# A fused attention and gated FFN kernel: VectorE in written order through the projections, powers instead of reciprocals, other places for pieces of work

## The chip, the cores and the metric

The kernel runs on one core of one Trainium2 chip. The metric is the device time of one execution in microseconds (us); below 1% differences matter here, since the kernel takes some 1,100 us. The core has five engines that run their own instruction streams and wait for each other by semaphores: TensorE (PE, with its weight loads as PEld), VectorE (DVE), ScalarE (ACT), GpSimd (POOL) and SyncE (SP, which here only issues DMAs). Tiles lie in SBUF as 128 partitions by some elements; matmul results land in PSUM banks of 128x512 floats.

## What is computed

```python
x   = hidden_states                      # (B, S, E) = (4, 512, 1024), float32
xn  = (x - mean) / sqrt(var + 1e-5)      # layernorm without gain
# attention: 16 heads of 64, rotary on all 64 dimensions, causal
q, k = rotary(xn @ Wq), rotary(xn @ Wk); v = xn @ Wv
attn = softmax(where(causal, q k^T, -1e9) / 8)
s    = (attn v) @ Wo
# gated FFN with signs of weights and scales chosen by a router over 8 experts
r    = softmax(xn @ gate_w^T)            # (B*S, 8)
out  = (xn * (r @ in_channel_scale)) @ sign(weight)^T * (r @ out_channel_scale) + bias
g    = silu(out)
result = x + s * g
```

## The kernel before

**Tiling.** Batches b = 0 to 3 go one after the other. The heads of a batch form 4 groups g, a group two units, `u = (b, g, i)` with i = 0, 1, of two heads each. For each group six tiles of 128 columns x 512 rows are projected: q and k of unit 0, q and k of unit 1, v of both. Their running number is the position `pos`, 24 to a batch. To keep float32 accuracy with the fast matmul type, an operand is split into two digits (high and low), and a tile is 24 products of 128x512 in three passes of eight: high weights by high x (`xh`), low by low (`xl`), and a mixed pass, `wm` by `xm`. The products are L364 in `passes`. The first 16 go to one PSUM bank, which ScalarE copies to `part` (L339), the last 8 to a second; VectorE adds both into `c` (L418; L414 for the last tile of a batch, which has another order). The projections' banks come from a ring of four. So a tile's bank is free again once ScalarE or VectorE has read it. From q and k the rotary embedding (`rotary`, L325 and L326 on VectorE, L327 and L328 on GpSimd) makes `rot`; v is transposed on TensorE (`turn_values`, L347, tile `vt`).

**Weights.** In batch 0 the raw float32 weights are loaded (`load_w`, issued by ScalarE, `wr<-in_wqkv`), and `digits_w` makes the high digit on ScalarE (step 0, L299), the low one on VectorE (step 1, L301), writes both to `w_d` in DRAM (issued by SyncE), and makes `wm` (step 2, L316 on VectorE; for odd positions from 13 to 23 L311 on ScalarE and L312 on GpSimd). Later batches load both digits from `w_d` (issued by GpSimd, L280, three buffers), and only `wm` is made again. `beside(n)` in `project` places these steps behind the n-th product of a tile.

**Beside the products.** A group has 144 products, and `interleave` calls "pieces" ahead of the products whose numbers are their keys. The pieces do the attention of the group before (`attention_pieces`): `scores` (L476), `softmax` (VectorE adds the mask and takes the maximum, L493; ScalarE takes the exponentials and their row sums, L505; VectorE their reciprocals, L514; GpSimd scales the rows, L516), `transpose_blocks` (ten VectorE transposes, L534, into a staging tile `y` that has one buffer, and 16 small DMAs `p<-y` issued by SyncE, L544, which bring it into the place of the probabilities), `values` (L559) and the store of its result, `at_d<-v`. Unit 0's scores stand at product 24, unit 1's at 96. In the last group of batch 3 the attention of the group before has places of its own. The pieces also do, for the next batch, the layernorm (`layernorm_scales` L174 and on, `normalize`), the transposes of x and their digits (`transpose_x`, `high_x` on ScalarE, `low_x` L238 on VectorE, `mixed_x`), the router (`router_tile`, `router_turn`, `router`), once in batch 0 the load and split of the FFN's scales `isc` and `osc` (`load_scales`, `split_scales`, L660 to L668), and in batch 3 the signs of the FFN's weights (`make_sign`).

**What sets the order.** TensorE runs in written order throughout (`manual_schedule(engines={PE})`); VectorE and ScalarE only in the start, before the first group. Elsewhere the scheduler of the framework orders the instructions of an engine when the program is built, but for those marked `keep_in_program_order`. On the chip each engine runs its stream in that built order, and an instruction that waits holds all behind it.

**After the groups** come the last units' attention, the FFN and the output projection (products L1156 and L1216), some 340 us. There `load_xn` loads normalized rows back by SyncE and, in four small loads by GpSimd each, the router's weights `RT` for a pair of row tiles; its first call stands in group 1 of batch 3.

## Time and profile before

| what | value |
|---|---|
| time, median of 3 runs | 1114.22 us (1111.3 to 1115.96) |
| profiled execution: its time, its span | 1117.55 us, 1115.8 us |
| mean granted TensorE clock | 0.986 |
| PE, PEld busy | 1069.3 us (96%), 734.8 us (66%) |
| DVE busy, instructions | 871.3 us (78%), 1857 |
| ACT busy, instructions | 391.1 us (35%), 931 |
| POOL busy, instructions | 548.9 us (49%), 642 |
| start to the first product of group 0 | 28.5 us |
| batch 0: groups 0 to 3 | 31.5, 48.1, 56.0, 60.3 us |
| batch 1 | 44.5, 43.4, 48.7, 49.0 us |
| batch 2 | 44.4, 43.4, 49.4, 47.5 us |
| batch 3 | 45.8, 45.5, 45.6, 46.0 us |
| after the last product | 777.5 to 1115.8 us |

A group's time goes from its first product of L364 to the next group's. (Group 0 of batch 0 has only four of its six tiles; the other two are made in the start.) Busy time of PE is modelled from pipelined matmuls, and it holds work at a lower clock too: the granted clock, 1.00 at full speed, says how much of a stretch PE ran at which speed. "x <- ENGINE y" behind an instruction gives its idle time and what ended it. An engine's waits cost time only where the engine is on the path that ends last; for this kernel that is, most of the time, PE's stream of products.

### The profile page before, as it was taken

Reading aid. Unit: us, or ns where it says so; the run is one execution under the profiler, and the core shown is the slowest. Engines: PE = TensorE matmul, PEld = TensorE weight load, DVE = VectorE, ACT = ScalarE, POOL = GpSimd, SP = SyncE. Lnnn points to the kernel's source line nnn. Section 1 sums busy time; section 2 is a strip of 40 time slices with the busy share of each in tenths; the row PEclk is TensorE's granted clock in tenths of the full one; section 3 lists DMA queues with packets and bytes.
Section 4 is the critical chain, followed back from the end, with each engine's and each line's share of the span. In section 5 each row is a group of like instructions: output and inputs, shape, how many; then the busy total and the mean of one; then the engine's idle time right before and its main releaser. Section 6 shows DMA issues by size and latency. Waiting matters only on the chain.

```text
span 1115.8 us, 15662 instructions
## 1 busy us (share of the span) xinstructions
PE 1069.3 (96%) x4948; PEld 734.8 (66%) x4948; DVE 871.3 (78%) x1857; ACT 391.1 (35%) x931; POOL 548.9 (49%) x642
## 2 busy tenths in 40 slices
PE   9897988899999999999999999999999999999998
PEld 8675665577776667776677766766654546655664
DVE  5989867787877898678888989978775876667663
ACT  4243645333343433324444223343530222222220
POOL 1545665644755546555464644654552333432334
PEclk9898989999999999999999999999999999999999
DMA  8686767898678787777778787686665223431331
GB/s 303 249 313 182 277 210 258 270 290 248 193 208 267 227 258 205 218 228 211 251 230 233 230 258 243 202 233 197 209 183 188 88 72 123 155 115 51 141 113 57
DMA packets 86530, 228.37 MB, mean 205 GB/s; under 512 B 14640, under 2 KB 37936, under 8 KB 74032
## 3 DMA queue, kind: packets, MB, share of 16 engines
q1 hardware_dynamic: 67408, 129.71, 37.7%
q0 software_dynamic: 15344, 85.60, 23.7%
q10 hardware_dynamic: 3696, 12.06, 3.1%
q8 instruction: 40, 0.66, 0.2%
q14 instruction: 42, 0.34, 0.1%
HBM read 134.77 MB, written 50.59 MB: 166 GB/s over the span
## 4 chain that ended last, share of the span: by engine, by line
PE 38%; DVE 22%; DMA 14%; SPq 8%; issue 5%; POOL 3%; ACT 3%; DVEq 0%; ACTq 0%; POOLq 0%
PE wo L1216 15%; PE pj L364 11%; SPq L544 7%; DVE y L534 7%; PE ff L1156 6%; DMA w<-w_d 5%; DMA p<-y 4%; DVE wm L316 3%; PE pv L559 2%; DMA at_d<-v 2%; DVE sc L493 2%; POOL p L516 2%; PE sc L476 2%; DVE c L418 2%; DVE rot L325 2%
## 5 line engine op out<-in xcount | busy, mean ns | idle before, releaser
L364 PE MATMUL pj<-xm,wm 128*128 128x512 f32 x752 | 202.5, 404 | 12.0 <-DVE c L418 7.2
L364 PE MATMUL pj<-xh,w 128*128 128x512 f32 x752 | 198.1, 404 | 5.6 <-DVE xl L238 4.9
L364 PE MATMUL pj<-xl,w 128*128 128x512 f32 x752 | 193.8, 396 | 0.0
L327 POOL TENSOR_TENSOR c<-c,sin_sb 128x512 f32<-128x512 f32 x64 | 89.1, 1392 | 208.7 <-DVE c L326 202.8
L516 POOL TENSOR_SCALAR p<-p,rs 128x256 f32<-128x256 f32 (+3 forms) x256 | 172.6, 686 | 34.9 <-DVE rs L514 23.6
L505 ACT ACTIVATE p<-sc,nmx 128x256 f32<-128x256 f32 (+3 forms) x256 | 133.3, 526 | 130.9 <-DVE nmx L493 73.9
L364 PEld LDWEIGHTS pj<-xh,w 128*128 128x128 f32 x752 | 140.2, 192 | 47.7 <-issue 8.8
L364 PEld LDWEIGHTS pj<-xm,wm 128*128 128x128 f32 x752 | 139.6, 192 | 43.7 <-DVE c L418 8.0
L316 DVE SCALAR_TENSOR_TENSOR wm<-w 128x1024 fp32r<-128x1024 f32 x88 | 128.0, 1454 | 44.7 <-DMA w<-w_d 24.7
L364 PEld LDWEIGHTS pj<-xl,w 128*128 128x128 f32 x752 | 140.5, 190 | 30.5 <-issue 1.6
L493 DVE CUSTOM_DVE_ANT_0 sc<-sc,mask 128x384 f32<-128x384 f32 (+3 forms) x256 | 121.4, 506 | 10.9 <-PE sc L476 9.1
L534 DVE STREAM_TRANSPOSE y<-p 128x256 f32<-128x256 f32 x320 | 107.9, 405 | 2.3 <-POOL c L327 1.2
L339 ACT ACTIVATE part<-pj 128x512 f32<-128x512 f32 x90 | 53.8, 598 | 146.6 <-PE pj L364 79.6
L328 POOL TENSOR_TENSOR rot<-rot,c 128x512 f32<-128x512 f32 x64 | 93.1, 1454 | 3.9
L559 PE MATMUL pv<-p,v 128*64 128x256 f32 (+3 forms) x512 | 79.1, 453 | 9.3 <-DMA p<-y 4.3
L476 PE MATMUL sc<-rot,rot 64*128 64x128 f32 (+3 forms) x512 | 79.5, 443 | 0.0
L559 PEld LDWEIGHTS pv<-p,v 128*64 128x64 f32 x512 | 36.4, 140 | 55.6 <-issue 40.4
L418 DVE TENSOR_TENSOR c<-pj,part 128x512 f32<-128x512 f32 x90 | 61.0, 678 | 12.8 <-PE pj L364 12.8
L280 POOL DMA_DIRECT2D w<-w_d x73 | 43.1, 590 | 53.6 <-PE pj L364 47.9
L476 PEld LDWEIGHTS sc<-rot,rot 64*128 64x128 f32 x512 | 42.4, 187 | 30.1 <-issue 21.0
L1216 PE MATMUL wo<-wo,ap 128*128 128x512 f32 x128 | 58.5, 599 | 0.0
L1236 POOL TENSOR_TENSOR xp_z<-xp_z,xr 128x512 f32<-128x512 f32 x16 | 22.8, 1423 | 66.9 <-DVE xp_z L1235 66.9
(186 smaller groups left out, 1582.4 us busy)
## 6 DMA issues: line engine op xcount, KB each, us to landing
w<-w_d POOLq DMA_DIRECT2D x73, 1024.0 KB, 6.3
p<-y SPq DMA_DIRECT2D x496, 80.0 KB, 2.7
w_d<-w SPq DMA_DIRECT2D x24, 1024.0 KB, 6.6
wr<-in_wqkv ACTq DMA_DIRECT2D x20, 512.0 KB, 5.5
at_d<-v SPq DMA_DIRECT2D x32, 256.0 KB, 5.4
ap<-at_d SPq DMA_DIRECT2D x16, 512.0 KB, 5.0
xr<-in_x SPq DMA_DIRECT2D x32, 256.0 KB, 2.9
xin<-in_x SPq DMA_DIRECT2D x12, 512.0 KB, 6.4
```

Of the source, the lines that this page charges most:

```text
L316: nc.vector.scalar_tensor_tensor(WM[key], low.bitcast(F32), -1.0 / LOW, hi.bitcast(F32), op0=ALU.mult, op1=ALU.add)
L327: nc.gpsimd.tensor_tensor(c, c, sin_sb, op=ALU.mult)
L328: nc.gpsimd.tensor_tensor(rot, rot, c, op=ALU.add)
L364: nc.tensor.matmul(ps, lhsT=wd[:, k, :], rhs=xd[:, k, :], start=(at == 0), stop=(at == n - 1),)
L418: nc.vector.tensor_tensor(c, second, p, op=ALU.add)
L476: nc.tensor.matmul(head(i, h), lhsT=Q[u][r : r + D, i * P : (i + 1) * P], rhs=K[u][r : r + D, : (i + 1) * P], start=True, stop=True,)
L493: nc.vector.tensor_tensor_reduce(out=ps[h], in0=ps[h], in1=mask[:, (TPB - 1 - i) * P :], scale=-SCALE, scalar=FAR, op0=ALU.add, op1=ALU.mi ...
L505: nc.scalar.activation(pt[:, h, :], ps[h], AF.Exp, bias=nmx[:, h : h + 1], scale=-1.0, accum_out=ssum[:, h : h + 1],)
L516: nc.gpsimd.tensor_scalar(pt[:, h, :], pt[:, h, :], rs[:, h : h + 1], 1.0, op0=ALU.mult, op1=ALU.mult,)
L534: nc.vector.transpose(out[:, :, :, o : o + 32], src.rearrange("p h (b c) -> p h b c", b=4))
L559: nc.tensor.matmul(by_block[r : r + D, :, 32 * j :], lhsT=V[u][:, j, r : r + D], rhs=PT[u][:, :, o : o + 32 * (TPB - j)], start=(j == 0), ...
L1216: nc.tensor.matmul(ps, lhsT=lhs[:, k, :], rhs=rhs[:, k, :], start=(first and k == 0), stop=(k == 3), skip_group_check=not first,)
```

## The change

The change has seven parts.

1. `interleave` of all groups runs under `manual_schedule(engines={DVE})`: VectorE's instructions of the projections keep the written order, with no scheduler. `beside` and the pieces are written accordingly: a tile's `c` is written right behind its last product; `ahead_of_scores` (rotary of the tile before, then `wm` of the next one) comes at the third product of a tile, or ahead of scores where these come first; `digits_w` steps 0 and 1 stay at 9 and 13; `mixed_x` goes to 10, 13, 16, 19.
2. `softmax` works on pairs of row tiles with a shared tile of row sums. Their reciprocals are no longer VectorE instructions, two to a pair, but one GpSimd power with exponent -1 over 128x4; the scaling follows for both tiles.
3. Places of attention: transposes of unit 1 at product 12 instead of 4, of unit 0 at 88 instead of 76 (last group 82 instead of 62), and in the last group those of unit 1 at 136 instead of 124.
4. Layernorm of the next batch: statistics and normalization of one tile at 8 and of the next at 62, instead of both statistics at 0 and normalization at 0 and 30; `low_x` comes 7 products behind its transposes.
5. The router's softmax is cut in two (steps 1 and 1.5) and its steps get other places.
6. The load and split of the scales move from group 1 of batch 0 (2, 52, 86) to group 0 of batch 1 (2, 66, 128).
7. The loads of `RT` keep the written order.

```diff
@@ -82,8 +82,9 @@
     nc.gpsimd.memset(eps, EPS)
-    power = cp.tile([P, 1], F32, name="power")
-    nc.gpsimd.memset(power, -0.5)
+    power = cp.tile([P, 2], F32, name="power")
+    nc.gpsimd.memset(power[:, 0:1], -0.5)
+    nc.gpsimd.memset(power[:, 1:2], -1.0)
@@ -180,7 +181,7 @@
         rstd = st.tile([P, 1], F32, tag="rstd", name=f"rstd_{b}_{t}")
         nc.gpsimd.tensor_tensor(rstd, mv[:, 1:2], eps, op=ALU.add)
-        nc.gpsimd.tensor_tensor(rstd, rstd, power, op=ALU.pow)
+        nc.gpsimd.tensor_tensor(rstd, rstd, power[:, 0:1], op=ALU.pow)
         MV[b, t] = mv, rstd
@@ -220,7 +221,6 @@
         if b > 0:
             high_x(b, t, g)
-            low_x(b, t, g)
         if g == 1:
@@ -348,8 +348,19 @@
             nc.scalar.copy(V[u], vt)
+    now = [0]
+    mixed = {2, 3}
+
+    def ahead_of_scores(pos):
+        while turn:
+            rotary(*turn.pop(0))
+        if pos + 1 not in mixed:
+            mixed.add(pos + 1)
+            digits_w(pos + 1, 2)
+
     def project(pos):
+        now[0] = pos
         key = b, g, m, i = keys[pos]
@@ -375,19 +386,16 @@
                 if pos + 2 == 23:
                     load_w(24)
-            if n == 3 and turn:
-                rotary(*turn.pop(0))
+            if n == 3:
+                ahead_of_scores(pos)
             if n == 20:
                 turn_values()
-            if last and b + 1 < B and n in (10, 12, 14, 16):
-                mixed_x(b + 1, (10, 12, 14, 16).index(n))
+            if last and b + 1 < B and n in (10, 13, 16, 19):
+                mixed_x(b + 1, (10, 13, 16, 19).index(n))
             if pos in (4, 5) and n in (6, 10):
                 digits_w(pos - 4, (6, 10).index(n))
-            if pos + 2 < 24:
-                if n in (9, 13, 18):
-                    digits_w(pos + 2, (9, 13, 18).index(n))
-            elif n == 12:
-                digits_w(pos + 2, 2)
+            if pos + 2 < 24 and n in (9, 13):
+                digits_w(pos + 2, (9, 13).index(n))
@@ -482,8 +490,12 @@
     def softmax(u, *tiles):
+        if len(tiles) > 2:
+            softmax(u, *tiles[:2])
+            return softmax(u, *tiles[2:])
         un = "%d_%d_%d" % u
-        for i in tiles:
+        ssum = st.tile([P, 2, 2], F32, tag="ssum", name=f"ssum_{un}_{tiles[0]}")
+        for n, i in enumerate(tiles):
             pt, ps = probs(u, i), SC[u, i]
@@ -500,7 +512,6 @@
                     accum_out=nmx[:, h : h + 1],
                 )
-            ssum = st.tile([P, 2], F32, tag="ssum", name=f"ssum_{un}_{i}")
             for h in range(2):
@@ -508,13 +519,16 @@
                     bias=nmx[:, h : h + 1],
                     scale=-1.0,
-                    accum_out=ssum[:, h : h + 1],
-                )
-            rs = st.tile([P, 2], F32, tag="rs", name=f"rs_{un}_{i}")
-            nc.vector.reciprocal(rs, ssum)
+                    accum_out=ssum[:, n, h : h + 1],
+                )
+        nc.gpsimd.tensor_tensor(
+            ssum, ssum, power[:, 1:2, None].to_broadcast((P, 2, 2)), op=ALU.pow
+        )
+        for n, i in enumerate(tiles):
+            pt = probs(u, i)
             for h in range(2):
                 nc.gpsimd.tensor_scalar(
-                    pt[:, h, :], pt[:, h, :], rs[:, h : h + 1], 1.0,
+                    pt[:, h, :], pt[:, h, :], ssum[:, n, h : h + 1], 1.0,
                     op0=ALU.mult, op1=ALU.mult,
@@ -610,6 +624,10 @@
             )
             nc.scalar.activation(exv, exv, AF.Exp)
+            R["ex"] = ex
+        elif step == 1.5:
+            ex = R["ex"]
+            exv = ex[:, :, :NE]
             ssum = st.tile([P, TPB], F32, tag="rsum", name=f"rsum_{b}")
@@ -627,7 +645,6 @@
             for n in (1, 0):
                 nc.vector.tensor_copy(ex[:, :, n * NE : (n + 1) * NE], hi)
-            R["ex"] = ex
         else:
@@ -698,9 +715,11 @@
         RT[q] = rtp.tile([P, 2, P], F32R, tag="rt", name=f"rt_{q}")
         for j in range(4):
-            nc.gpsimd.dma_start(
-                out=RT[q][32 * j : 32 * j + 32, :, :],
-                in_=rt_d[b, t : t + 3 : 2].rearrange("t e p -> e t p"),
+            tc.keep_in_program_order(
+                nc.gpsimd.dma_start(
+                    out=RT[q][32 * j : 32 * j + 32, :, :],
+                    in_=rt_d[b, t : t + 3 : 2].rearrange("t e p -> e t p"),
+                )
             )
@@ -835,6 +854,7 @@
                 if before:
                     values(before)
+                ahead_of_scores(now[0] + 1)
                 scores(u)
@@ -844,15 +864,15 @@
         last = k == len(groups) - 2
         plan = {
-            4: lambda: v and transpose_blocks(v),
+            12: lambda: v and transpose_blocks(v),
             24: values_and_scores(w, u0),
             32: lambda: softmax(u0, 2, 0),
-            62 if last else 76: lambda: transpose_blocks(u0),
+            82 if last else 88: lambda: transpose_blocks(u0),
             72 if last else 96: values_and_scores(v, u1),
...
         }
         if last:
-            plan[124] = lambda: transpose_blocks(u1, ordered=True)
+            plan[136] = lambda: transpose_blocks(u1, ordered=True)
         return {n: [piece] for n, piece in plan.items()}, units
@@ -876,25 +896,27 @@
                         at(n + 14 * (t // 2), lambda f=f, t=t: f(0, t))
             else:
-                at(56, lambda: router(b, 1))
+                at(44, lambda: router(b, 1))
+                at(54, lambda: router(b, 1.5))
                 at(74, lambda: router(b, 2))
+            if b == 1:
+                at(2, lambda: (load_scales(in_scale), load_scales(out_scale)))
+                at(66, lambda: split_scales(isc))
+                at(128, lambda: split_scales(osc))
         elif g == 1 and b + 1 < B:
             at(100, lambda: [load_x(b + 1, t) for t in range(2)])
             if b == 0:
-                at(2, lambda: (load_scales(in_scale), load_scales(out_scale)))
-                at(12, lambda: router(0, 1))
-                at(34, lambda: router(0, 2))
-                at(52, lambda: split_scales(isc))
-                at(86, lambda: split_scales(osc))
+                at(10, lambda: router(0, 1))
+                at(20, lambda: router(0, 1.5))
+                at(44, lambda: router(0, 2))
         elif g > 1 and b + 1 < B:
             t0 = 2 * (g - 2)
-            layernorm_scales(b + 1, t0)
-            layernorm_scales(b + 1, t0 + 1)
-            normalize(b + 1, t0)
-            at(30, lambda: normalize(b + 1, t0 + 1))
+            for n, t in ((8, t0), (62, t0 + 1)):
+                at(n, lambda t=t: (layernorm_scales(b + 1, t), normalize(b + 1, t)))
             for n, t, h in ((46, t0, 0), (56, t0, 1), (108, t0 + 1, 0), (116, t0 + 1, 1)):
                 at(n, lambda t=t, h=h: transpose_x(b + 1, t, h))
+                at(n + 7, lambda t=t, h=h: low_x(b + 1, t, h))
             at(78, lambda: router_tile(b + 1, t0))
@@ -915,7 +937,8 @@
             if g == 2:
                 at(8, lambda: in_scales(0, score_banks))
-        interleave(pieces, fill, 0 if k else 2 * 3 * NC, 6 * 3 * NC)
+        with tc.manual_schedule(engines={DVE}):
+            interleave(pieces, fill, 0 if k else 2 * 3 * NC, 6 * 3 * NC)
         if g == NGRP - 1:
             for _ in fill:
                 pass
```

## The prediction

> **What bounds the kernel now.** First I read the windows, cut at each group's first projection product (L364): below, groups 1 to 3 of batch 0, then groups 0 to 3 of batch 1, 144 products each. Columns: stretch, its length, busy time of PE, PEld, DVE, ACT and POOL with counts, granted clock, DMA share, GB/s.
>
> ```profile
> core 0: us, PE busy (x) PEld busy (x) DVE busy (x) ACT busy (x) POOL busy (x), PEclk, DMA share, GB/s
> 59.90:108.00 48.10, 42.42 (x186) 32.44 (x185) 44.97 (x91) 18.95 (x44) 27.52 (x29) 0.93 0.71 239
> 108.00:164.00 56.00, 50.53 (x250) 36.01 (x250) 44.60 (x99) 30.54 (x66) 35.97 (x37) 0.94 0.76 248
> 164.00:224.30 60.30, 51.44 (x267) 36.50 (x266) 45.60 (x100) 27.99 (x61) 33.53 (x36) 0.94 0.78 255
> 224.30:268.80 44.50, 44.50 (x236) 32.82 (x235) 36.64 (x98) 15.29 (x44) 25.26 (x31) 1.00 0.84 261
> 268.80:312.20 43.40, 43.40 (x218) 32.37 (x217) 33.16 (x84) 14.85 (x42) 24.36 (x30) 1.00 0.77 225
> 312.20:360.90 48.70, 47.54 (x251) 34.48 (x250) 39.50 (x95) 20.96 (x53) 25.97 (x36) 1.00 0.75 232
> 360.90:409.90 49.00, 48.06 (x268) 34.44 (x267) 41.87 (x99) 21.29 (x54) 25.77 (x35) 1.00 0.76 233
> ```
>
> The same products take 164.4 us in batch 0 (first three rows) and 141.1 in batch 1 (last three), with the clock at 0.93 to 0.94 against 1.00. From batch 1 on, PE is the bound: products start 0.227 us apart (48 in 10.9 us in the chain). Next, what PE waits for between 59 and 224:
>
> ```profile
> PE pj L364 <- DVE c L418: 7.2, 2, 5.7
> PE pj L364 <- DVE xl L238: 5.8, 2, 3.1
> PE pv L559 <- DMA p<-y: 4.3, 1, 4.3
> ```
>
> With three smaller rows (1.4, 0.7, 0.7) that is 20.1 us. Columns are sum, times, longest. The timeline of DVE shows what stood ahead of the sum c in the longest wait, 91.9 to 97.5:
>
> ```profile
> 93.85 0.71 DVE L666 TENSOR_SCALAR xin<-xin,row_kind 128x1024 f32<-128x1024 f32 x1
> 94.48 1.22 DVE L316 SCALAR_TENSOR_TENSOR wm<-w 128x1024 fp32r<-128x1024 f32 x1
> 95.61 1.28 DVE L668 SCALAR_TENSOR_TENSOR osc<-osc,row_kind,xin 128x1024 fp32r<-128x1024 f32 x1
> 96.81 0.68 DVE L418 TENSOR_TENSOR c<-pj,part 128x512 f32<-128x512 f32 x1
> ```
>
> The split of the scales and the next-but-one wm run first (ten transposes, 3.36 us, before them); the tile's last pass was long done. So in batch 0 PE waits for the order on DVE, not for its capacity: DVE is busy 44.6 of 56.0 and 45.6 of 60.3. From 224 to 750 PE waits only 8.9 us in all, 4.9 of them vt for c.
>
> **The change, part by part.** Sums are made in the profiled execution (1117.55 us, span 1115.8, 1.75 outside it) and taken off the median, 1114.22; the 3.3 between them I leave alone.
>
> *Batch 0, groups 1 to 3.* Three things leave DVE or move. The split, 0.69+0.75+2.29 for isc, 0.68+0.71+1.28 for osc and 0.45 of row kinds, 6.85 us, leaves group 1. The reciprocals leave: in all 128 of 163 ns with 40.1 us of waiting in front of them, of which the sum behind an eviction waits too. c comes ahead of wm (1.2 to 1.5 us). In written order transposes of unit u1 (piece 12) also stand before the next softmax; before, DVE did the one at 184.33 after it, its 16 transfers were issued up to 203.5 and the value product waited 4.3. Floors: PE as in batch 1, 43.4 less two value products of 2.3 that group 1 hasn't, 38.8, then 48.7 and 49.0, sum 136.5; DVE 44.97-6.85-1.2=36.9, 43.3, 44.3, lower in each. Ceiling 164.4-136.5=28. That agrees with the 20.1 of waits plus the half clock: five rows of 25 us from 75 to 225 show 0.93, 0.94, 0.86, 0.93, 0.93, that is 0.41x25=10.2 us. But both engines are nearly full, w L301 still waits for raw weights (w L301 <- ACT w L299, 4.1 in one wait at 101), and DVE now can't step around that. I take two thirds, **18** (8 to 28).
>
> On the clock: each PE wait of 2.6 us or more up to 224 (5.7, 2.6, 3.1, 4.3) is followed by 3.4 or 6.8 us at 0.50; after 830 a wait of 2.57 is too. *The Trainium skill, "TensorE: Matmul & The Clock Gate", section HAM oscillation, warns of idle gaps above about 3.4 us alone; by it only the 5.7 and the 4.3 would cost clock, 5 of the 10.2 us; here shorter waits cost too, and the row decides.*
>
> *Powers on GpSimd.* Two for each unit, 64. No 128x4 power is in the trace; nearest row rstd L183, 128x1, 556 ns. Lower bound 0.556, upper four times that; I take 0.6, 38 us in all, 2.4 of the 43 to 60 of a group where POOL is busy 24 to 36. Queued behind one: the scaling L516, rotary's L327 and L328, and weight loads w<-w_d. Scaling now waits for two tiles' exponentials, some 1.7 us later; the cover is that transposes of u0 stand at product 88 instead of 76, 56 products or 12.7 us after the second softmax. At the upper price 4 powers add 9 us to a group's POOL, 35 of 43: still hidden, save 1 us a group if loads slip (0 to 13, taken 0).
>
> *The Trainium skill, "SBUF — State Buffer", section Who interferes with whom, says that a VectorE instruction with two SBUF inputs and a GpSimd one that reads SBUF block each other for the whole instruction. The trace agrees in kind: isc L668 took 2.29 us beside a busy POOL and osc L668 1.28. By the rule at its worst the 38 us of powers would all be added to DVE, 2.4 a group; the windows leave DVE 7 to 10 there, so the sum stays as it is.*
>
> *Batch 1, group 0* takes the split: DVE 36.64+6.85-1.2=42.3 of 44.5. Two loads of 0.5 MB (4 us at 261 GB/s) go on SP ahead of p<-y and at_d there. Cost 0 to 4, taken 1.
>
> *Other groups.* wm(pos+1) now comes after c, rotary's two DVE steps and before the scores. DVE waited 19.2 us in 10 times with wm for PE (224 to 750), each with the sum behind it; those end. low_x seven products after its transposes and statistics one tile at a time remove head waits of 1.5 us. Of the 8.9 us that PE waited I take 4 (0 to 9).
>
> *The loads of rt* (8 on POOL, 0.56 each) move from 77 us to batch 3 and the tail: 2.2 us each where POOL idles (11.1 us before 787). Taken 0 (-1 to 1).
>
> *The last group* goes the wrong way. Transposes of u0 move from product 62 to 82, behind the second softmax; those of u1 from 124 to 136. Both write one staging tile y, freed when its 16 transfers have landed. Before:
>
> ```profile
> 758.49 3.38 DVE L534 STREAM_TRANSPOSE y<-p 128x256 f32<-128x256 f32 x10
> ...
> 762.01 10.09 SPq L544 DMA_DIRECT2D p<-y  x16
> ...
> 774.83 3.38 DVE L534 STREAM_TRANSPOSE y<-p 128x256 f32<-128x256 f32 x10 [1.18 <-POOL c L327]
> ...
> 779.18 0.66 PE L347 MATMUL vt<-ident,c 128*128 128x128 f32 x4 [1.31 <-DVE c L414]
> ```
>
> Start to start 16.3 us, with 1.18 of idling. After: scores end at 760.8, two softmaxes 3.6 us (starts 743.62 to 748.94 less 1.7 of waits), so u0's transposes start at 764.5 and u1's not before 780.8; ten of them 3.3, then the last sum c 0.7, which stands behind: vt at 784.8 instead of 779.2. 5.6 us, and by the rows above some 1.7 us of half clock. I take **7** (0 to 9).
>
> Sum: -18+1-4+7 = -14; 1114.2-14 = **1100**.
>
> **The rivals.** *All waits go* (A): batch 0 reaches its floor (-28), other groups -8, last group +3: 1081. For: DVE has room in every row. Against: written order makes every late input a late sum.
>
> *Batch 0 is held by its loads* (B): the raw weights (5.5 us landing, DMA share 0.71 to 0.78) set L301, L301 the sum. Then only the split and some reciprocals count, -8, others 0, last +7 and +1: 1114, no change. For: w L301 <- ACT w L299 and wr<-in_wqkv in the chain (195.9, 5.2 us). Against: batch 1 moves as many GB/s without waits.
>
> *The staging tile holds DVE in every group* (C, slower): u0's transposes at 88 and u1's at 12 are 68 products apart, 15.4 us plus 4.7 of value product and scores, 20.1. A cycle takes 3.4+transfers+2.7 landing. From 14.0 us of transfers on, DVE stands with the sum behind it. Rows: 10.1 to 11.0 in batch 3, 15.8 once in batch 0. If 15.8 holds everywhere, 1.8 us in each of 26 unit turns, half of it reaching PE with its clock, 27: 1114-14+27=1127.
>
> *It doesn't take effect* has no place: the built order differs on DVE from the third projection on.
>
> **How the numbers follow.** Forecast 0.55 (own range 1090 to 1109), A 0.15, B 0.18, C 0.12. The range 1084 to 1116 takes in the forecast, a little of A and most of B. A measurement here tells about 0.5%, 5.6 us, from no change: faster is A, nearly all of the forecast and a third of B, 0.76; same 0.13; slower C's most, 0.11.
>
> **What would show it.** Right: groups 1 to 3 of batch 0 take some 146 us, with PEclk 1.00 in most of 75 to 225; no split at 80 to 97 but in batch 1; vt <- c of about 6 us at the end of the projections, half clock after it. Wrong: DVE idle before L301 in batch 0 (B); y L534 <- DMA p<-y on DVE in many groups (C); no vt wait at the end (A, or my cycle of y is too long); powers far above 0.6 us with POOL the bound.

## The result, and the profile after

The changed kernel takes 1162.66 us (median of 4 runs, 1162.05 to 1165.88) against 1114.20 of the kernel before: ratio 1.0443, 95% interval 1.0414 to 1.0473. The change makes it 4.4% slower; the prediction was 1100, and its range ended at 1116. In the profiled execution the span is 1160.8 us against 1115.8, the mean granted clock 0.976 against 0.986. DVE is as busy as before (871.9 us against 871.3), POOL much busier: 656.2 against 548.9.

Where the 45.0 us went is read from the first products (now L375) of the groups and a few later marks of TensorE's stream, which has nearly the same order in both kernels:

| stretch, us | before | after | difference |
|---|---|---|---|
| batch 0 | 195.9 | 194.4 | -1.5 |
| batch 1 | 185.5 | 192.9 | +7.4 |
| batch 2 | 184.8 | 189.7 | +4.9 |
| batch 3 | 182.9 | 196.8 | +13.9 |
| last product to last vt | 1.7 | 6.4 | +4.7 |
| vt to first product of the output projection | 54.1 | 56.6 | +2.5 |
| from there to the last product | 278.0 | 290.8 | +12.8 |

Table and windows come from one execution of each kernel. The windows of the changed kernel at the same places as in the prediction: groups 1 to 3 of batch 0, then 0 to 3 of batch 1 (columns as there).

```profile
core 0: us, PE busy (x) PEld busy (x) DVE busy (x) ACT busy (x) POOL busy (x), PEclk, DMA share, GB/s
57.50:103.70 46.20, 42.48 (x186) 31.95 (x185) 39.87 (x85) 18.94 (x47) 28.74 (x23) 0.93 0.76 267
103.70:159.00 55.30, 49.51 (x251) 35.26 (x250) 43.61 (x91) 30.02 (x63) 42.63 (x43) 0.94 0.70 239
159.00:222.90 63.90, 53.35 (x267) 37.48 (x266) 47.20 (x93) 26.82 (x60) 41.66 (x39) 0.92 0.84 273
222.90:268.50 45.60, 44.69 (x235) 32.65 (x234) 39.49 (x96) 14.78 (x44) 27.65 (x30) 1.00 0.73 225
268.50:314.00 45.50, 43.60 (x218) 32.39 (x217) 37.16 (x79) 14.53 (x42) 33.80 (x37) 1.00 0.71 212
314.00:367.40 53.40, 47.93 (x251) 34.58 (x250) 38.34 (x87) 20.42 (x53) 36.12 (x46) 1.00 0.76 220
367.40:415.80 48.40, 47.72 (x267) 34.69 (x266) 40.54 (x91) 20.91 (x54) 32.46 (x37) 1.00 0.78 239
```

POOL has 7 to 10 us more in five of these seven groups. In batch 0 the clock is no better. In batch 1, where PE was busy almost without a break, it now has gaps: in group 2 53.40 of length against 47.93 busy, where it was 48.70 against 47.54. What PE waits for over the whole execution, and what DVE waits for (sum, times, longest):

```profile
PE pj L375 <- DVE c L426: 15.6, 9, 4.5
PE lt L611 <- ACT lgs L605: 8.5, 5, 3.1
PE vt L347 <- DVE c L422: 6.0, 1, 6.0
...
PE is L738 <- DMA rt<-rt_d: 4.6, 14, 1.0
```

```profile
DVE sc L505 <- ACT p L516: 49.0, 32, 3.5
...
DVE wm L316 <- DMA w<-w_d: 27.0, 12, 4.9
```

The 38.9 us that DVE waited in front of its reciprocals before are not gone:

```profile
DVE rs L514 <- ACT p L505: 38.9, 56, 1.1
```

Instead 49.0 us now stand in front of the mask addition of row tile 0, which shares a PSUM tile with row tile 2 and, in written order, waits until ScalarE has read it.

The last group, on its timeline, went as predicted:

```profile
795.48 7.34 SPq L558 DMA_DIRECT2D p<-y  x10
...
804.73 3.38 DVE L548 STREAM_TRANSPOSE y<-p 128x256 f32<-128x256 f32 x10 [5.77 <-DMA p<-y]
...
808.04 0.66 DVE L422 SCALAR_TENSOR_TENSOR c<-pj,part 128x512 f32<-128x512 f32 x1
...
808.75 1.12 PE L347 MATMUL vt<-ident,c 128*128 128x128 f32 x4 [6.04 <-DVE c L422]
```

Unit 1's transposes wait 5.77 us for the staging tile, the last sum stands behind them, and PE waits 6.04 us for it.

### The profile page after: what moved, and what is told of

Its sections match the earlier page's. It is cut to its first block, busy times and chain, and to the rows that moved or that the text cites. A ratio compares the mean times of both kernels' runs of the same rounds, so it can differ in the third digit from the quotient of the medians.

```text
span 1160.8 us, 15591 instructions
## 1 busy us (share of the span) xinstructions
PE 1086.2 (94%) x4948; PEld 742.0 (64%) x4948; DVE 871.9 (75%) x1729; ACT 385.4 (33%) x931; POOL 656.2 (57%) x707
## 4 chain that ended last, share of the span: by engine, by line
PE 26%; DVE 22%; POOL 15%; DMA 14%; issue 13%; SPq 5%; ACT 4%; POOLq 0%; ACTq 0%; DVEq 0%
PE pj L375 14%; DVE y L548 6%; POOL p L530 5%; DMA p<-y 5%; SPq L558 4%; PE wo L1239 4%; DMA w<-w_d 4%; PE pv L573 3%; PE sc L484 2%; ACT p L516 2%; DVE sc L505 2%; DVE wm L316 2%; DMA wr<-in_wqkv 2%; POOL z_t L1259 2%; DVE rot L325 1%
## 5 line engine op out<-in xcount | busy, mean ns | idle before, releaser
L375 PE MATMUL pj<-xh,w 128*128 128x512 f32 x752 | 202.1, 410 | 21.7 <-DVE c L426 13.4
L375 PE MATMUL pj<-xm,wm 128*128 128x512 f32 x752 | 206.9, 409 | 14.3 <-POOL wm L312 5.7
L327 POOL TENSOR_TENSOR c<-c,sin_sb 128x512 f32<-128x512 f32 x64 | 119.4, 1866 | 152.6 <-DVE c L326 152.6
L375 PE MATMUL pj<-xl,w 128*128 128x512 f32 x752 | 193.8, 396 | 0.0
L375 PEld LDWEIGHTS pj<-xh,w 128*128 128x128 f32 x752 | 142.1, 195 | 65.8 <-DVE c L426 16.9
L530 POOL TENSOR_SCALAR p<-p,ssum 128x256 f32<-128x256 f32 (+3 forms) x256 | 176.9, 710 | 5.4
L505 DVE CUSTOM_DVE_ANT_0 sc<-sc,mask 128x256 f32<-128x256 f32 (+3 forms) x256 | 122.9, 510 | 67.1 <-ACT p L516 49.0
L375 PEld LDWEIGHTS pj<-xm,wm 128*128 128x128 f32 x752 | 142.0, 195 | 45.6 <-issue 7.6
L375 PEld LDWEIGHTS pj<-xl,w 128*128 128x128 f32 x752 | 140.9, 190 | 30.4 <-issue 1.4
L316 DVE SCALAR_TENSOR_TENSOR wm<-w 128x1024 fp32r<-128x1024 f32 x88 | 116.9, 1328 | 27.1 <-DMA w<-w_d 27.0
L524 POOL TENSOR_TENSOR ssum<-ssum,power 128x4 f32<-128x4 f32 x64 | 73.1, 1143 | 72.0 <-ACT p L516 66.5
L328 POOL TENSOR_TENSOR rot<-rot,c 128x512 f32<-128x512 f32 x64 | 88.2, 1378 | 4.3
L426 DVE TENSOR_TENSOR c<-pj,part 128x512 f32<-128x512 f32 x90 | 60.9, 677 | 27.7 <-PE pj L375 23.7
L325 DVE TENSOR_TENSOR rot<-c,cos_sb 128x512 f32<-128x512 f32 x64 | 60.3, 943 | 2.0
```

What stands on the lines that cost most here:

```text
L316: nc.vector.scalar_tensor_tensor(WM[key], low.bitcast(F32), -1.0 / LOW, hi.bitcast(F32), op0=ALU.mult, op1=ALU.add)
L325: nc.vector.tensor_tensor(rot, c, cos_sb, op=ALU.mult)
L327: nc.gpsimd.tensor_tensor(c, c, sin_sb, op=ALU.mult)
L328: nc.gpsimd.tensor_tensor(rot, rot, c, op=ALU.add)
L375: nc.tensor.matmul(ps, lhsT=wd[:, k, :], rhs=xd[:, k, :], start=(at == 0), stop=(at == n - 1),)
L505: nc.vector.tensor_tensor_reduce(out=ps[h], in0=ps[h], in1=mask[:, (TPB - 1 - i) * P :], scale=-SCALE, scalar=FAR, op0=ALU.add, op1=ALU.mi ...
```

## The experiments

Each was measured beside runs of the kernel before on the same chip; ratios are against these. Lengths of stretches are from each run's trace, as in the table above.

**The loads of RT.** In the changed kernel's timeline, at one of the last five pairs of row tiles:

```profile
932.86 1.26 POOL L1024 TENSOR_TENSOR xp_z<-xp_z,bias_sb 128x512 f32<-128x512 f32 x1 [0.63 <-DVE xp_z L1023]
...
934.06 2.18 POOL L719 DMA_DIRECT2D rt<-rt_d  x4
...
936.11 0.38 PE L738 MATMUL is<-rt,isc 32*128 32x256 f32 x1 [0.96 <-DMA rt<-rt_d]
```

The four loads are issued behind the bias addition, 2 us before they are needed. In the kernel before, the loads for the same pair were issued 68 us ahead of the first product that reads them:

```profile
872.94 2.17 POOL L701 DMA_DIRECT2D rt<-rt_d  x4 [0.84 <-PE os L749]
...
941.41 0.51 PE L719 MATMUL is<-rt,isc 32*128 32x256 f32 x8
```

Run e1, the changed kernel with `tc.keep_in_program_order(...)` around these loads removed. 

> The changed kernel without its seventh part: the loads of RT (four small ones by GpSimd for each pair of row tiles) are free for the scheduler again. Theory: in written order they stand behind GpSimd's bias additions of the stage before, are issued about 2 us late, and each of the six pairs of row tiles after 930 us waits for them; the gaps between the two kernels grow by 13.0 us there (31.9 to 44.9). Freed, the kernel takes 1162.7-13 = 1149.7 us, and no matmul of in_scales (L738) waits for rt<-rt_d. Rival: the tail is longer because everything ahead of it, stores and staged tiles too, arrives later; then freeing the loads gives back under 3 us, 1160 or more.

Measured: ratio 1.0383 (1.0342 to 1.0425), 1159.29 us. In the place predicted it is exact: from the output projection's first product to its last 278.0 us again, and TensorE waits for no RT load. But its projections end 10.9 us later in the profile (813.2 against 802.3 us), so the total expected was missed. Batch 0, in which the first eight of these loads now stand again, is 2.4 us longer. The rest is mainly in the first groups of batches 2 and 3 (5.1 and 4.3 us longer), in which no instruction stands in another order than in the changed kernel. The timelines of the first of these show what differs. First the changed kernel, then e1, whose group begins 3.1 us later:

```profile
437.46 0.85 DVE L635 TENSOR_TENSOR rex<-rex,rrs 128x32 f32<-128x32 f32 x1
...
438.34 0.52 DVE L640 CAST rhi<-rex 128x32 fp32r<-128x32 f32 x1
...
439.92 0.33 PE L650 MATMUL rt<-ident,rex 128*128 128x128 f32 x1 [0.86 <-DVE rex L647]
```
```profile
440.07 2.00 DVE L635 TENSOR_TENSOR rex<-rex,rrs 128x32 f32<-128x32 f32 x1
...
440.61 1.28 POOL L327 TENSOR_TENSOR c<-c,sin_sb 128x512 f32<-128x512 f32 x1
...
441.88 1.89 POOL L530 TENSOR_SCALAR p<-p,ssum 128x384 f32<-128x384 f32 x4
...
442.10 2.94 DVE L640 CAST rhi<-rex 128x32 fp32r<-128x32 f32 x1
...
443.75 1.25 POOL L328 TENSOR_TENSOR rot<-rot,c 128x512 f32<-128x512 f32 x1
...
445.64 0.48 PE L650 MATMUL rt<-ident,rex 128*128 128x128 f32 x1 [3.46 <-DVE rex L647]
```

For the first 18 us of the group DVE, ACT and POOL run alike in both, to 0.1 us. Then L325 on DVE and a scaling on POOL start within 0.03 us of each other; in the changed kernel the first takes 1.21 us and the second 0.70, in e1 0.69 and 1.20. From there POOL is half a microsecond later, small steps of the router on DVE (L635, L640) lie beside a power, L327, scalings and L328 and take 2.00 and 2.94 us instead of 0.85 and 0.52, TensorE waits 3.46 us for them instead of 0.86, and 6.8 us at half clock follow. In batch 3 two of these steps (L635, L643) take 2.02 and 2.46 us in e1 instead of 0.85 and 0.53, and the wait is 3.95 us instead of 0.87. So in these groups the loss comes with GpSimd's work beside VectorE's, in the same order of instructions; what shifted the two against each other is not shown.

Run e6, the converse in the kernel before. 

> The kernel before with the loads of RT kept in written order, nothing else. Theory: the tail from the first product of the output projection to the end takes 290.8 us instead of 278.0, as in the changed kernel; without the seventh part it took 278.0 again: 1114+13 = 1127. Rival: the 12.8 us need the changed kernel's later arrivals: 1114 to 1117.

```diff
-            nc.gpsimd.dma_start(out=RT[q][...], in_=rt_d[...])
+            tc.keep_in_program_order(nc.gpsimd.dma_start(out=RT[q][...], in_=rt_d[...]))
```

Measured: ratio 1.0100 (1.0065 to 1.0134), 1129.8 us; that stretch takes 290.7 us. Seven parts of the change, and this one alone costs 1%. (In e6's profile batch 0, which no longer holds the first eight loads, is 5.0 us shorter than before, but that is the fastest of its eight executions.)

**Powers, pairs and the written order.** Run e2, the changed kernel without the written order. 

> The changed kernel without the written order of VectorE in the groups: the scheduler orders it, all places of pieces stay as changed. Theory: batches 1 to 3 lose 26.2 us because in written order each late input (the maximum of row tile 0 behind ScalarE's exponentials, 34.9 us of waits there; wm behind weights; signs of weights) holds the sum c and with it TensorE; with the scheduler two thirds of it, 17 us, come back and 5 of the 6.0 us in which the last transposes of v wait: 1140. Rival: the loss is GpSimd's, busy 656 us against 549, through powers of 1.14 us that delay scalings and layernorm; then the order on VectorE matters little and it stays at 1155 to 1165.

```diff
-        with tc.manual_schedule(engines={DVE}):
-            interleave(pieces, fill, 0 if k else 2 * 3 * NC, 6 * 3 * NC)
+        interleave(pieces, fill, 0 if k else 2 * 3 * NC, 6 * 3 * NC)
```

Measured: 1.0321 (1.0280 to 1.0362), 1152.38 us: 10 us back, not 23, and at 65.0 us instead of 27.0 DVE now waits for weights (wm behind w<-w_d). Neither number fits "the order alone".

Run e5, the other half alone: the changed `softmax` and `power` in the kernel before. 

> The kernel before with the changed softmax alone (pairs of row tiles, one GpSimd power of 128x4 in place of the reciprocals), VectorE ordered by the scheduler, all places as before. Theory: the powers are what costs most. They take 1.14 us each, 73 us in all, and GpSimd stands in front of them 66 us waiting for exponentials, with the loads of weights queued behind (GpSimd's wait for a free weight buffer fell from 46.5 to 15.0 us, so the loads are issued some 30 us later in sum): 1114+20 = 1134, and VectorE's wait of wm for w<-w_d grows well above 24.7 us. Rival: the written order on VectorE is what costs, and GpSimd has room for the powers (busy 549 of 1116): 1110 to 1119.

Measured: 1.0503 (1.0460 to 1.0547), 1174.09 us, at least as slow as the whole change. DVE's wait for weights is 109.4 us. One such case on the timeline:

```profile
680.43 3.50 POOL L523 TENSOR_SCALAR p<-p,ssum 128x256 f32<-128x256 f32 x4
...
683.88 0.64 POOL L281 DMA_DIRECT2D w<-w_d  x1
...
684.54 1.15 POOL L517 TENSOR_TENSOR ssum<-ssum,power 128x4 f32<-128x4 f32 x1
...
685.80 1.85 POOL L523 TENSOR_SCALAR p<-p,ssum 128x384 f32<-128x384 f32 x4
...
692.07 1.23 DVE L317 SCALAR_TENSOR_TENSOR wm<-w 128x1024 fp32r<-128x1024 f32 x1 [6.54 <-DMA w<-w_d]
...
693.22 0.68 DVE L419 TENSOR_TENSOR c<-pj,part 128x512 f32<-128x512 f32 x1
```

The load is issued behind the first pair's scaling, wm waits 6.54 us for it, and the sum c stands behind wm.

Run e9 parts pairing from power: as e5, but with one VectorE reciprocal of 128x4 for a pair. 

> The kernel before with the softmax in pairs and one VectorE reciprocal of 128x4 for each pair; no powers, all else as before. It parts the power from the pairing in the run before, which cost 57 us. If the power itself costs (1.12 us each on GpSimd, with loads of weights queued behind), this kernel is back near the one before: 1114 to 1122. If the pairing costs (GpSimd's scaling of the first tile waits for the exponentials of the second, the loads behind it too), most of the 57 us stays: 1145 to 1175.

```diff
-        nc.gpsimd.tensor_tensor(ssum, ssum, power[:, 1:2, None].to_broadcast((P, 2, 2)), op=ALU.pow)
+        nc.vector.reciprocal(ssum, ssum)
```

Measured: 1.0113 (1.0074 to 1.0151), 1128.87 us: between the two expectations, nearer to the first. Pairing alone costs 13 us.

Run e12 adds the powers alone, without pairs and beside the reciprocals. 

> The kernel before, reciprocals and all, with 64 powers more: for each pair of row tiles one GpSimd power of 128x4 into a tile that nobody reads, ready when the reciprocal is. It doubles the suspected cost alone: 1.12 us of GpSimd 64 times, without any pairing and without the wait for a second tile. If occupation of GpSimd is what costs: 1135 to 1160. If the wait at the head of GpSimd's queue costs, not the power: 1114 to 1122.

```diff
             nc.vector.reciprocal(rs, ssum)
+            if i in (3, 0):
+                idle = st.tile([P, 2, 2], F32, tag="idle", name=f"idle_{un}_{i}")
+                nc.gpsimd.tensor_tensor(idle, rs[:, :, None].to_broadcast((P, 2, 2)),
+                    power[:, 0:1, None].to_broadcast((P, 2, 2)), op=ALU.pow)
```

Measured: 1.0196 (1.0151 to 1.0241), 1138.39 us. So 64 powers that nobody waits for cost 22 us; occupation of GpSimd costs by itself. By which way is the next question. DVE's waits of wm in the kernel before, with pairs (e9), with idle powers (e12) and with both (e5):

```profile
DVE wm L316 <- DMA w<-w_d: 24.7, 12, 4.5
```
```profile
DVE wm L317 <- DMA w<-w_d: 61.2, 19, 7.5
```
```profile
DVE wm L316 <- DMA w<-w_d: 76.4, 28, 6.4
```
```profile
DVE wm L317 <- DMA w<-w_d: 109.4, 24, 7.7
```

The waits rise in the order of the losses: 0, 13, 22, 57 us. The sum of the single losses is 35, so some 20 come from pair and power together; no run parts them further.

Two tests whether the loads behind the powers are the way. Runs e15 and e16 load the weights' digits by SyncE, with and without idle powers. 

> The kernel before with 64 idle powers, and the loads of the weights' digits issued by SyncE instead of GpSimd. To be read against the same loads without powers (next run). Theory: powers cost because loads of weights are queued behind them on GpSimd (VectorE's wait of wm for w<-w_d went 24.7, 61.2, 76.4, 109.4 us with 0, 13, 22, 57 us of loss); with the loads in another queue the powers cost under 6 us. Rival: the powers cost through scalings and rotary embeddings on GpSimd, which stay behind them: 15 to 25 us more than the next run.

> The kernel before with the loads of the weights' digits issued by SyncE, nothing else: the control of the run with idle powers. GpSimd loses 43 us of issuing; SyncE's small transfers of probabilities stand behind loads that wait for a free buffer. If those matter: 1120 to 1140; if not, 1105 to 1116 with a shorter wait of wm than 24.7 us.

```diff
-            nc.gpsimd.dma_start(out=WH[key].rearrange(...), in_=w_d[g, m, i])
+            nc.sync.dma_start(out=WH[key].bitcast(F32).rearrange(...), in_=w_d[g, m, i].bitcast(F32))
```

Measured: e15 1.0598 (1.0553 to 1.0643), e16 1.0500 (1.0447 to 1.0553): the control itself is 5% slower, since the loads stand in SyncE's queue behind its other waits (in e16 158.5 us for the transposes y alone; TensorE waits 36 us for w<-w_d in both). The powers cost 12 us there, between the two expectations. Inconclusive.

Run e17 keeps powers and pairs and turns the queue round. 

> The kernel before with the changed softmax (pairs and powers, 57 us slower), and GpSimd's queue turned round: loads of the weights' digits and powers keep written order, the load at product 18 of a tile, the powers and scalings of both pairs of a unit at 44 and 116 (92 in the last group), so that each load is issued ahead of the powers it stood behind. The powers, their pairs and their number stay. Theory (powers act through the loads behind them): VectorE's wait of wm for w<-w_d falls from 109.4 to below 40 us and the time from 1174 to 1120-1140. Rival (they act through later scalings and rotary embeddings, or by blocking VectorE): 1155 or more.

```diff
+            if n == 18 and pos >= 24:
+                load_w(pos + 3)
...
-            32: lambda: softmax(u0, 2, 0),
+            32: lambda: second(u0),
+            44: lambda: finish_both(u0),
```

Here `second` makes maxima and exponentials only, and `finish_both` the powers and scalings of both pairs.

Measured: 1.0376 (1.0349 to 1.0403), 1158.86 us, in the rival's range; DVE's wait is 61.2 us and not below 40. So the theory's two numbers were missed. The stretches say where. From the first product to group 1 of batch 1, e5 loses only 1 us against the kernel before and e17 loses 20; there TensorE waits 8.0 us in one piece for a copy on ScalarE. From group 1 of batch 1 to the last product of batch 3:

| kernel | stretch, us | DVE's wait of wm for w<-w_d in it, us |
|---|---|---|
| before | 508.7 | 23.7 |
| pairs (e9) | 524.7 | 54.8 |
| idle powers (e12) | 532.0 | 69.7 |
| pairs and powers (e5) | 561.5 | 104.8 |
| the same behind the loads (e17) | 523.2 | 48.1 |

Here three quarters of e5's loss (38.2 of 52.8 us) go, and in all four runs the loss is 50 to 65% of what the wait grew by. That speaks for the load behind the power as the main way in these groups. It is not shown alone, since e17 moves the powers and scalings to other products too. What holds the earlier groups in e17, perhaps the later scalings, was not tested.

Run e7, the changed kernel with reciprocals in place of the powers. 

> The changed kernel with the power of each pair replaced by one VectorE reciprocal of 128x4 in the same place, everything else as changed. If the powers on GpSimd cost most (theory), GpSimd loses 73 us of work and its weight loads come early again: 1163-20 = 1143. If the written order costs most (rival), VectorE now also waits in it for the exponentials of both pairs, some 2 us 64 times, with the next sum behind: 1165 to 1185.

```diff
-        nc.gpsimd.tensor_tensor(ssum, ssum, power[:, 1:2, None].to_broadcast((P, 2, 2)), op=ALU.pow)
+        nc.vector.reciprocal(ssum, ssum)
```

Measured: 1.0450 (1.0390 to 1.0511), 1168.88 us: no gain, though the powers are gone. DVE now waits 77.4 us for exponentials in front of the reciprocals and 41.9 in front of mask additions. Here the rival was right, as the theory was in e5: either is enough for a loss of this size, and in the changed kernel the two do not add up.

**Late inputs in the written order.** Run e3 puts the maxima of both tiles ahead. 

> The changed kernel with the mask additions and maxima of both row tiles of a pair ahead of the exponentials of both, in VectorE's and ScalarE's written order. It takes away the wait of VectorE for ScalarE between the two tiles (L505 behind L516: 49.0 us in 32 waits). Theory: these waits hold the sum behind them and about half of TensorE's 15.6 us of waits for c L426 goes with them: 1163-8 = 1155, and VectorE's wait for L516 falls below 5 us. Rival: a softmax of products 32 and 104 ends well before the next sum, at 48 and 120, so that the 1.5 us are absorbed: 1160 to 1165 though the waits are gone.

```diff
+            NMX.append((pt, ps, nmx))
+        for n, (pt, ps, nmx) in enumerate(NMX):
             for h in range(2):
                 nc.scalar.activation(
```

Measured: 1.0420 (1.0373 to 1.0468), 1164.16 us: the 49.0 us of waits are gone and the time is the same. The rival's number was right; instead DVE waits for the next late thing, weights (50.4 us).

Run e4 moves the normalizations. 

> The changed kernel with the normalization of the next batch's tiles 22 products behind their statistics (30 and 84 instead of 8 and 62). Theory: ScalarE's normalization waits for GpSimd's reciprocal deviation, which stands behind powers, scalings and a rotary embedding there (7.3 us in one wait at 187 to 194.5 us), and holds the eviction, the high digits and the router's copies behind it: TensorE's 8.5 us of waits of L611 for L605 and the 6.6 us of VectorE's low digits L301 in group 3 of batch 0 end: 1163-10 = 1153. Rival: the wait only moves, since GpSimd's work in front stays: 1160 to 1165.

```diff
-                at(n, lambda t=t: (layernorm_scales(b + 1, t), normalize(b + 1, t)))
+                at(n, lambda t=t: layernorm_scales(b + 1, t))
+                at(n + 22, lambda t=t: normalize(b + 1, t))
```

Measured: 1.0505 (1.0451 to 1.0559), 1174.42 us, worse by 12 us. The theory fell: TensorE still waits 9.5 us for the router's copies. The wait it was drawn from is real (timeline of the changed kernel below, group 3 of batch 0), but a later place only hands it on: in e4 ScalarE waits for the deviations as long as before (72.9 us in all against 73.8).

```profile
194.56 1.24 ACT L195 ACTIVATE xin<-xin,mv,rstd 128x1024 f32<-128x1024 f32 x1 [7.32 <-POOL mv L187]
...
198.92 1.06 ACT L299 ACTIVATE w<-wr 128x1024 fp32r<-128x1024 f32 x1
...
200.06 1.23 DVE L301 TENSOR_TENSOR w<-wr,w 128x1024 fp32r<-128x1024 f32 x1 [6.59 <-ACT w L299]
...
204.58 0.67 DVE L426 TENSOR_TENSOR c<-pj,part 128x512 f32<-128x512 f32 x1
```

Reading it downwards: ScalarE stands 7.32 us for a deviation that is behind powers and scalings on POOL, its high digits come late, DVE waits 6.59 us for them, and c comes after that.

Runs e10 and e11 put reciprocals on VectorE, behind their exponentials; e11 also frees the RT loads and takes the old places in the last group. 

> The changed kernel with three edits to the softmax: maxima of both tiles ahead of the exponentials, VectorE reciprocals of 128x4 instead of powers, and each pair's reciprocal and scaling 8 to 10 products behind its exponentials (32 and 42, 104 and 114; in the last group 80 and 90). So VectorE's written order holds no wait for ScalarE. If the written order costs only through such waits and the powers cost the rest (theory), batches 1 to 3 come to 185 us each: 1163-24 = 1139. If the written order is slower in itself, through signs, transposes and weights ahead of the sum (rival): 1155 to 1165.

> The run before (deferred reciprocals) with the loads of RT free for the scheduler, and in the last group the transposes at 62 and 124 as before instead of 82 and 136. Theory: 12.8 us of the tail and some 5 us of the wait for the last sum go: 18 less than the run before, 1121 if that takes 1139. Rival: in the projections the freed loads and early transposes, which now wait for scalings, take as much: within 5 us of the run before.

```diff
-            32: lambda: softmax(u0, 2, 0),
+            32: lambda: second(u0),
+            42: lambda: rest[u0, 2](),
...
-            82 if last else 88: lambda: transpose_blocks(u0),
+            62 if last else 88: lambda: transpose_blocks(u0),
```

Here `second` first finishes pair 1 and then makes maxima and exponentials of pair 2, which 42 finishes; the last two lines are e11's.

Measured: e10 1.0334 (1.0289 to 1.0378), 1153.36 us; e11 1.0178 (1.0129 to 1.0226), 1135.19. The step from e10 to e11 is the 18 us expected (tail 292.6 to 278.0, vt 7.0 to 1.3). But e10 did not test its theory: a later product number moves nothing on an engine that has no work between, and DVE waited 101.4 us for the exponentials all the same.

Run e13 puts both reciprocals behind the next sum, where there is work between. 

> The changed kernel with free loads of RT, maxima first, VectorE reciprocals instead of powers, and both reciprocals and scalings of a unit behind the next sum: at products 50 and 122 (98 in the last group), its transposes there at 76 and 130. In the run with reciprocals at 32 and 42 VectorE had nothing between them and waited 101 us for the exponentials all the same. Theory (written order costs through late inputs only): VectorE's wait of the reciprocal falls below 10 us, batches 1 to 3 come to 186 us each, total 1112 to 1122. Rival (the written order costs in itself, by what stands ahead of the sum): batches 1 to 3 stay at 189 to 197 us and the total at 1128 to 1140.

```diff
             32: lambda: second(u0),
+            50: lambda: finish_both(u0),
...
+            98 if last else 122: lambda: finish_both(u1),
```

Measured: 1.0076 (1.0046 to 1.0107), 1122.66 us, the theory's range missed by less than 1 us. Batches 0 to 3: 187.9, 188.7, 188.2 and 186.5 us, so batches 1 to 3 lie between the theory's 186 and the rival's 189 to 197. From e11 it differs only in the places of reciprocals and scalings and of the last group's transposes, and it is some 12 us faster. No wait of TensorE's products for c L426 is left in batches 1 to 3, and DVE waits less for the late inputs, if not below 10 us for the exponentials:

```profile
DVE ssum L535 <- ACT p L519: 17.7, 17, 1.4
...
DVE wm L316 <- DMA w<-w_d: 8.2, 8, 1.9
```

Run e14 moves three more pieces. 

> The run before this one with three more places moved away from a sum or a TensorE piece that follows closely: the router's last step 94 instead of 74, its reduction of the fourth tile (router_turn) 42 instead of 26, make_sign 36 instead of 60 with its load at 6. Theory: TensorE's waits for rex, row_kind and ltg (14 us in the run with reciprocals at 32 and 42) and those behind the signs in batch 3 go: 10 to 15 less than that run. Rival: each place only hands its 5 to 7 us of VectorE to the next sum: within 5 us of it.

```diff
-                at(74, lambda: router(b, 2))
+                at(94, lambda: router(b, 2))
...
-            at(26, lambda: router_turn(pb + 1, 2 * (pg - 2) + 1))
+            at(42, lambda: router_turn(pb + 1, 2 * (pg - 2) + 1))
...
-            at(60, lambda: make_sign(n))
+            at(36, lambda: make_sign(n))
```

Measured: 1.0113 (1.0069 to 1.0158), 1125.62 us: not told apart from e13, as the rival had it. In its profile, the fastest of its four executions, batches 1 to 3 take 188.1, 185.8 and 182.3 us, close to the kernel before. So with fewer late inputs the written order costs little; in the totals of e13 and e14, which hold the moved scales too, it brings nothing either. The new places of layernorm and router are in both and were not tested alone.

**The scales.** Run e8, the kernel before with the scales in batch 1. 

> The kernel before with the loads and the split of the scales moved from group 1 of batch 0 to group 0 of batch 1 as in the change, nothing else. Prediction: 6.85 us of VectorE's work leaves batch 0, where it stood ahead of a late sum, and the half clock after the wait goes: batch 0 is 7 us shorter, batch 1 1 us longer, 1108. Rival: VectorE's order in batch 0 is set by the weights' digits that wait for ScalarE (L301 behind L299), so that the room is filled by another wait: 1112 to 1117.

```diff
-                at(2, lambda: (load_scales(in_scale), load_scales(out_scale)))
-                at(52, lambda: split_scales(isc))
-                at(86, lambda: split_scales(osc))
+            if b == 1:
+                at(2, lambda: (load_scales(in_scale), load_scales(out_scale)))
+                at(66, lambda: split_scales(isc))
+                at(128, lambda: split_scales(osc))
```

Measured: 0.9974 (0.9948 to 0.9999), 1114.7 us. In the profile group 1 of batch 0 takes 40.7 us instead of 48.1, the 7 us expected, and batch 0 187.2; over the runs 3 us remain (the interval goes from nearly 0 to 6), and the total is in the rival's range. The profiled execution is the second fastest of ten.

Run e18 adds to it the removal of two loads that the kernel makes twice. 

> The kernel before with the scales moved to batch 1 (ratio 0.9974 alone) and, in the last group of batch 0, without two loads that are made twice there: the raw weights of position 23 (0.5 MB) and the digits of position 24 (1 MB). Theory: that group is held by its loads, so it loses 2 to 5 us of its 60: 1105 to 1110. Rival: the second loads go into spare buffers and delay nobody: 1110 to 1114, as with the scales alone.

```diff
-            if n == 2:
-                load_w(pos + (3 if pos + 3 < 24 else 2))
-                if pos + 2 == 23:
-                    load_w(24)
+            if n == 2 and pos != 22:
+                load_w(pos + (2 if pos > 22 else 3))
```

Measured: 0.9943 (0.9922 to 0.9963), 1109.27 us. Group 3 of batch 0 takes 56.8 us against 60.3 before and 59.6 in e8. It beats both kernels, by 0.6% and 4.6%. Over the runs it is not told apart from e8, so what the two loads cost is not shown.

## Why the prediction was wrong

The sum was 14 us faster; the profiles show 45 slower. Of the 59 us between them some 19 lie in groups 1 to 3 of batch 0, 29 in the other groups and 13 in the loads of RT; group 0 of batch 0 gives 2.5 back.

*Batch 0, "I take two thirds, 18": measured a loss of 1.* Groups 1 to 3 take 165.4 us against 164.4; only group 0, which the term left out, is 2.5 shorter. The part of the term for the split was about right in the profile: 7.4 us in group 1 in e8, though 3 over the runs. With the same powers but the scheduler's order batch 0 takes 185.7 us (e2), and in written order without the late reciprocals 187.9 (e13), against 195.9. So in these profiles some 8 to 10 us were to be had, most of them the split's, and not 18; and the written order took them back. In group 1, 46.2 us against 40.0 in e2, TensorE waits 1.92 us at 92.08 for a sum that stands behind ten transposes, and 6.8 us at half clock follow. Group 3, where the chain from POOL over ScalarE to L301 stands, is 3.6 us longer than before. Rival B's place was right (DVE waits 12.4 us for L299 in groups 1 to 3, 7.8 before), its cause, the loads, only in part: the normalization is ahead of them in that chain.

*Powers, "Taken 0 (0 to 13)": the step that failed first.* The duration was inside its bounds, 0.556 to four times that, but taken at the lower end: 0.6 against 1.14 us measured. More important, the prediction named the weight loads as queued behind a power and then costed them by POOL's busy share, 35 of 43. e12 shows what that leaves out: 64 idle powers cost 22 us on an engine half idle, and DVE's wait for weights rises from 24.7 to 76.4 us: POOL's idle time does not lie where the loads wait. And "scaling now waits for two tiles' exponentials, the cover is 56 products" covered the transposes, not the loads: pairing costs 13 us (e9), pair and power 57 (e5). These are prices in the scheduler's order; in the changed kernel reciprocals in place of the powers gain nothing (e7): DVE then waits 77.4 us in front of them.

*"Other groups, I take 4": measured a loss of 25* (26.2 in batches 1 to 3, of which 1.1 in group 0 of batch 1). DVE's waits with wm for PE did end, but inputs that the scheduler had worked around now hold the sum: exponentials (49.0 us) and weights. Besides, VectorE's work is longer where GpSimd works beside it, and in written order the sum stands behind that too. One case from batch 3 on the timeline:

```profile
771.54 1.62 POOL L524 TENSOR_TENSOR ssum<-ssum,power 128x4 f32<-128x4 f32 x1
...
772.19 2.63 DVE L694 TENSOR_SCALAR sg<-raw 128x512 fp32r<-128x512 f32 x1
...
773.15 1.26 POOL L327 TENSOR_TENSOR c<-c,sin_sb 128x512 f32<-128x512 f32 x1
...
774.40 2.12 POOL L530 TENSOR_SCALAR p<-p,ssum 128x384 f32<-128x384 f32 x4
...
774.86 3.45 DVE L695 SCALAR_TENSOR_TENSOR sg<-raw,sg 128x512 fp32r<-128x512 f32 x1
...
776.50 1.25 POOL L328 TENSOR_TENSOR rot<-rot,c 128x512 f32<-128x512 f32 x1
...
778.23 0.41 DVE L694 TENSOR_SCALAR sg<-raw 128x512 fp32r<-128x512 f32 x1
...
778.68 0.69 DVE L695 SCALAR_TENSOR_TENSOR sg<-raw,sg 128x512 fp32r<-128x512 f32 x1
...
779.29 0.68 DVE L426 TENSOR_TENSOR c<-pj,part 128x512 f32<-128x512 f32 x1
...
780.02 2.11 PE L375 MATMUL pj<-xh,w 128*128 128x512 f32 x8 [2.44 <-DVE c L426]
```

Signs written at product 60 take 7.2 us, and the sum and then TensorE wait. No wait stands in front of them, so their input is not late. The first two steps take 6.1 us beside a power, rotary's products and scalings on POOL, the same two steps after those 1.1.

The argument against rival A, "written order makes every late input a late sum", was the rule; the forecast did not apply it to batches 1 to 3. e13 gives the other side: with reciprocals on VectorE, free loads of RT and fewer late inputs in the order, no product there waits for c any more.

*"The loads of rt, taken 0 (-1 to 1)": measured 12.8* in the profile, shown from both sides (e6 in the kernel before, e1 and e11 in the changed one). The step counted what POOL spends on issuing, 2.2 us, and not that a load held in written order loses its lead: from 68 us ahead of its use, in the pair above, to 2.

*The last group, 7: right*, by the wait predicted (5.77 us for the staging tile). vt comes 6.4 us after the last product instead of 1.7, and the value products behind it, with half clock, lose 2.5 more: 7.2. With the old places vt comes after 1.3 us (e11, against 7.0 in e10).

*Batch 1, group 0, 1: right* (45.6 against 44.5 us). *Rival C* did not happen: DVE waits for the staging tile's transfers 5.8 us, once. The forecast, A and B all left GpSimd out as a bound, and no rival had it as one; only the last of the signs of being wrong named it. So the size and the sign of the time were missed together: the one rival that was slower, C, was so for another reason.

## What to carry to other kernels

An engine that issues loads is priced by what stands in front of each load when it could go, not by its busy share: GpSimd, half idle here, still had no room for a microsecond at that place. Before an engine is put into written order, list every input that can be late on it, and put real work, not product numbers, between producer and consumer (e10 and e11 against e13). And a load that is pinned "to keep it in order" should be looked up on the timeline: how long ahead of its use is it issued now, and how long then?

## What was not expected of the hardware

A GpSimd power of 128x4 takes 1.04 us in the median, one of 128x1 0.56. In total the 64 powers did not slow VectorE by blocking it: in e5 DVE is busy 850.9 us, 20.4 less than before, and the reciprocals that left were 20.9; with idle powers and all reciprocals (e12) it is busy 861.2 us against 871.3. That speaks against the prediction's worst case by the Trainium skill, "SBUF — State Buffer", section Who interferes with whom. The same section (whichever of VectorE and GpSimd has the shared ports first holds them for the whole instruction) does agree with single rows. In the changed kernel rotary's multiplication L327 stands beside wm in 44 of 64 cases, and 43 of the 64 take over 1.7 us, against 6 before (mean 1.87 against 1.39 us). The sign L694 above took 2.63 us and ended 0.41 us, its time alone, after L327 had: a power and then L327 were in front of it. And in e1 small steps of the router took 2.00 and 2.94 us beside work of GpSimd.

The clock after waits was less regular than the prediction had it: in the changed kernel waits of TensorE of 1.92, 2.65 and 3.12 us, which end at 92.1, 134.2 and 537.1, went with 6.8, 6.8 and 3.4 us at half clock, and one of 2.79 us that ends at 347.3 did not (granted clock 1.00 in the window of 314 to 367 above).
